# One block of bins for both image pairs in turn: head weights in six buffers, transfers in a fixed order, and the mix of images moved between blocks

## The chip, the cores and the metric

The kernel runs on one core of one Trainium2 chip. The metric is the device time in microseconds from launch to end; the figure quoted for a kernel is the median of several runs. Engines are named as in the profile: PE (TensorE matmuls), PEld (its weight loads), DVE (VectorE), ACT (ScalarE), POOL (GpSimd), SP (SyncE, here only the issuer of DMA transfers).

## The reference

Two layers follow one another, each added to its input. The first is a selective scan over a 48 × 48 image in four directions; the change does not touch it. The second is a spectral attention layer over an input of 4 batches × 48 images ("T") of 48 × 128 points with 32 heads. Cut to what matters:

```python
xa_n = inorm(x.reshape(B*T, 1, H, W))
k = fno_layer(xa_n, wK, wKs, bKs, (H//2, W//2))       # 32 heads each
q = fno_layer(xa_n, wQ, wQs, bQs, (H//2, W//2))
v = fno_layer(xa_n, wV, wVs, bVs, (H, W))
scores = einsum('bhtd,bhsd->bhts', qs, ks) / sqrt(d)
attn_w = softmax(scores, axis=-1)
out   = einsum('bhts,bhsd->bhtd', attn_w, vs)          # every head: a mix of the 48 images
projd = fno_layer(out, wP, wPs, bPs, (H, W))           # and back from 32 heads to one
attention = inorm(projd + xa)
...                                                    # two more spectral layers, norms, residual
# fno_layer(x): spectral part: multiply the low bins of rfft2(x) by complex weights, sum over heads;
#               plus a pointwise part: ws * x + bs
```

Since all of `v` and `projd` is linear in `xa_n`, the kernel never forms `v`. For each low bin n it computes, over heads h and images s, the sum of `attn[h,t,s] * g[h,n] * x[s,n]`, where `g` joins the weights of V and P, and x is the spectrum of the normalized image. The pointwise parts of V and P together are a 48 × 48 matrix for each batch, the "mix of images" (`a0_bd`): the sum over heads of `attn[h,t,s] * wPs[h] * wVs[h]`.

## The kernel before

The program is built with a tile framework. Tiles come from pools with a number of buffers per tag; a tile's first writer waits for the last readers of the buffer that it takes. Instructions issued through `nc` are put in order, engine by engine, by the framework's planner, which goes by program order and by its own estimate of when things become ready. Instructions issued through `on` (class `Ordered`, line 36) keep the order of the program among themselves on their engine; the helper's line 50 is therefore the line of all of them in the profile. Before the change `Ordered` knows TensorE, VectorE, ScalarE and GpSimd, not SyncE.

The second layer, `layer1` (line 735), begins with loads of constants and of the first layer's result. Line 916 opens the pool `l1_mid`, which holds the attention weights `attn_c` from the softmax to the end of the heads' stage. While statistics and the first transform run, `dgt` in DRAM is written (lines 1108 to 1115): the joint weights g of the 32 heads, for each of four blocks of 384 bins, real part, imaginary part and their sum. One block's transposes are copied by ScalarE into `gtt` (four tiles, one per block) and stored by SyncE. Later `keys` (line 1212) writes the images' spectrum to `dxt` in DRAM in the same blocks. The scores (line 1254) run at the same time; the softmax (lines 1273 to 1300) ends in transposes into `attn_c`, with (head, image s) on the partitions.

The heads' stage is lines 1308 to 1406. Its loops run over `pair` (2; a pair is two batches), `k` (4 blocks of 384 bins), `q` (3 groups of 16 images s) and `g` (4 groups of 8 heads). One (pair, k) is called a block here, one (pair, k, q) a step, one (pair, k, q, g) a group. The 128 partitions of a group are 16 images × 8 heads:

- `grep`: g of 8 heads at the block's bins, repeated for 16 images, 128 × 1152 values, one DMA transfer of 576 KB from `dgt` (line 1364). It is loaded at q = 0 and used by all three q of its block. The pool `l1_qg` has 4 buffers, the four g of one block.
- `xrep`: the spectrum of 16 images for both batches of the pair, each row repeated for 8 heads: two transfers of 576 KB from `dxt` (line 1356) for each step, two buffers.
- ScalarE copies two thirds of `grep` to PSUM (`gp`, line 1371); VectorE multiplies it by `xrep` into `v` (line 1373); GpSimd multiplies the last third into `v3` (line 1377; the profile calls it v too). Both have two buffers.
- TensorE multiplies by `attn_c` and sums over all q and g into three accumulators `acc` (line 1381): 6 matmuls of 64 columns a group, which the profile records as 12.

After 12 groups a block ends: ScalarE copies `acc[0]` to `s1` (1389), VectorE forms `zt` (1392 to 1394), TensorE transposes it in two lots of four (`pz`, 1399), ScalarE copies each to `z2` (1402). The accumulators have one buffer each, so the next block's matmuls need them read.

At the head of the stage, lines 1317 to 1327 load `wpv` (both pointwise weights of the heads, eight small transfers) and `mask` (three), and multiply the weights. `e_w` (1331, 1332) is built from them, and the mix of images is made for both pairs (1335 to 1348): 24 matmuls each into the PSUM tile of tag "tr", which `pz` uses as well, and a copy to `a0_bd`. Its result is first used in the next stage, the inverse transform.

The order of the transfers on SyncE's queue is the planner's. `grep` can be requested when the last step of the block before has used the buffer.

Of the kernel before, what the change touches and what calls it, by code (L numbers as in the profile page):

```python
# [10 lines left out]
F32 = mybir.dt.float32  # L11
# [8 lines left out]
B, T, H, W = 4, 48, 48, 128  # L20
# [9 lines left out]
NH = 32  # L30
# [5 lines left out]
class Ordered:  # L36


    def __init__(self, tc):
        for name in ("tensor", "vector", "scalar", "gpsimd"):  # L40
            setattr(self, name, _OrderedEngine(tc, getattr(tc.nc, name)))


# [691 lines left out]
def layer1(ctx, tc, io, x1_dram, out):  # L735
# [5 lines left out]
    nc = tc.nc  # L741
# [10 lines left out]
    on = Ordered(tc)  # L752
# [156 lines left out]
    NC = 384  # L909
# [7 lines left out]


    attn_c = pm.tile([128, B, 4, 3, 64], F32, name="attn_c")
    dxt = dram.tile([B, 4, T, 3 * NC], F32, name="dxt")  # L920


# [136 lines left out]
    with ExitStack() as ph:  # L1059
# [17 lines left out]
        with ExitStack() as pw:  # L1077
# [28 lines left out]
            on.vector.tensor_add(gw[:, :, 2], gw[:, :, 0], gw[:, :, 1])  # L1106

            for k in range(4):
                gt = q1.tile([NH, 3, NC], F32, name=f"gtt{k}")
                for c in range(3):  # L1110
                    p = ps_t.tile([128, 512], F32, tag="tr", name=f"pgt{k}_{c}")
                    for j in range(3):
                        on.tensor.transpose(p[0:NH, j * 128 : (j + 1) * 128], gw[:, 3 * k + j, c], ident)
                    on.scalar.copy(gt[:, c], p[0:NH, 0:NC])
                nc.sync.dma_start(dgt[k], gt.rearrange("h c n -> h (c n)"))
# [192 lines left out]
    with ExitStack() as ph:  # L1308
        p1 = ph.enter_context(tc.tile_pool(name="l1_q1", bufs=1))
        p2 = ph.enter_context(tc.tile_pool(name="l1_q2", bufs=2))  # L1310
        pg = ph.enter_context(tc.tile_pool(name="l1_qg", bufs=4))
        ps_t = ph.enter_context(tc.tile_pool(name="l1_qt", bufs=1, space=PSUM))
        ps_g = ph.enter_context(tc.tile_pool(name="l1_qp", bufs=2, space=PSUM))
        ps_y = ph.enter_context(tc.tile_pool(name="l1_qy", bufs=1, space=PSUM))


        wpv = p1.tile([128, 2, 4], F32, name="wpv")
        mask = p1.tile([128, 3, T], F32, name="mask")
        for c, n in enumerate(("wPs", "wVs")):
            w = io[n].rearrange("a b -> (a b)")  # L1320
            for g in range(4):
                nc.sync.dma_start(wpv[:, c, g : g + 1], w[8 * g : 8 * g + 8][None].to_broadcast([16, 8]))
        for q in range(3):
            nc.sync.dma_start(
                mask[:, q], io["c_ident"][16 * q : 16 * q + 16, 0:T][:, None].to_broadcast([16, 8, T])
            )
        nc.vector.tensor_mul(wpv[:, 0], wpv[:, 0], wpv[:, 1])
        e_w = []
        for g in range(4):
            e = p1.tile([128, 3, 3 * T], F32, tag=f"e_w{g}", name=f"e_w{g}")  # L1330
            nc.gpsimd.memset(e, 0.0)
            nc.vector.tensor_scalar(e[:, :, T : 2 * T], mask, wpv[:, 0, g : g + 1], None, ALU.mult)
            e_w.append(e)
        for pair in range(2):
            p = ps_t.tile([128, 512], F32, tag="tr", name=f"pa0{pair}")
            for i in range(2):
                o = p[0:96, i * T : (i + 1) * T]
                for gq in range(12):
                    g, q = divmod(gq, 3)
                    nc.tensor.matmul(  # L1340
                        o,
                        e_w[g][:, q, (1 - i) * T : (1 - i) * T + 96],
                        attn_c[:, 2 * pair + i, g, q, 0:T],
                        start=(i == 0 and gq == 0),
                        stop=(gq == 11),
                        skip_group_check=True,
                    )
            nc.scalar.copy(a0_bd[:, pair], p[0:96, 0:96])
        for pair in range(2):
            for k in range(4):  # L1350
                acc = [ps_y.tile([128, 512], F32, tag=f"acc{c}", name=f"acc{pair}_{k}_{c}") for c in range(3)]
                gr = []
                for q in range(3):
                    x = p2.tile([128, 2, 3, NC], F32, tag="xrep", name=f"xrep{pair}_{k}_{q}")
                    for b in range(2):
                        nc.sync.dma_start(
                            x[:, b].rearrange("p c n -> p (c n)"),
                            dxt[2 * pair + b, k, q * 16 : q * 16 + 16][:, None].to_broadcast([16, 8, 3 * NC]),
                        )
                    for g in range(4):  # L1360
                        t = f"{pair}_{k}_{q}_{g}"
                        if q == 0:
                            r = pg.tile([128, 3, NC], F32, tag="grep", name=f"grep{t}")
                            nc.sync.dma_start(
                                r.rearrange("p c n -> p (c n)"),
                                dgt[k, 8 * g : 8 * g + 8][None].to_broadcast([16, 8, 3 * NC]),
                            )
                            gr.append(r)
                        r = gr[g]
                        gp = ps_g.tile([128, 2, 512], F32, tag="gp", name=f"gp{t}")  # L1370
                        nc.scalar.copy(gp[:, :, 0:NC], r[:, 0:2])  # L1371
                        v = p2.tile([128, 2, 2, NC], F32, tag="v", name=f"v{t}")
# [6 lines left out]
                        for c in range(3):  # L1379
                            for b in range(2):  # L1380
# [4 lines left out]
                                    start=first,  # L1385
                                    stop=last,
                                )
                s1 = p2.tile([128, NC], F32, tag="s1", name=f"s1{pair}_{k}")
                nc.scalar.copy(s1, acc[0][:, 0:NC])  # L1389
                zt = p2.tile([128, 8, 2, 48], F32, tag="zt", name=f"zt{pair}_{k}")  # L1390
                a1, a2, a3 = (v[:, 0:NC].rearrange("p (k y) -> p k y", y=48) for v in (s1, acc[1], acc[2]))
# [3 lines left out]
                for k4 in range(2):  # L1395
                    p = ps_t.tile([128, 512], F32, tag="tr", name=f"pz{pair}_{k}_{k4}")
                    for i in range(4):
# [5 lines left out]
                        z2[pair][:, 8 * k + 4 * k4 : 8 * k + 4 * k4 + 4].rearrange("p k (b t) -> p k b t", b=2),  # L1403
                        p[0:96].rearrange("p (k b t) -> p k b t", b=2, t=64)[:, :, :, 0:T],
                    )
    mid.close()


# [553 lines left out]
```

## Time and profile before

| What | Value |
|---|---|
| Median of 3 runs | 5021.46 us (5015.16 to 5022.86) |
| Profiled execution, its own time | 5017.78 us |
| Its span, first to last instruction | 5016.0 us |
| Mean TensorE clock granted | 0.933 |
| Scores end, heads' stage begins | about 4441 us |
| First / last `acc` product of the heads' stage | 4477.6 / 4740.5 us |
| Busy over the span: PE, DVE, POOL, ACT | 83%, 83%, 80%, 59% |
| `xrep` transfers (576 KB each) | 48 |
| `grep` transfers (576 KB each) | 32 |

Times in the profile are microseconds from the first instruction. A row of instructions names line, engine, operation and output<-inputs; in brackets stands the idle time of the engine before it and what ended it. A row of waits gives who waited for whom, the total, how often, and the longest. The chain is the work that ended last, followed backwards through what released each piece. The clock is TensorE's granted clock as a share of full speed.

### The profile page before, as it was taken

To read this page: it belongs to the slowest core of one execution; us is meant where nothing else is said; L and a number is where in the kernel's file an instruction comes from. 1 tells how busy PE (TensorE), PEld (TensorE's weight loads), DVE (VectorE), ACT (ScalarE), POOL (GpSimd) and SP (SyncE) were. 2 spreads that over 40 slices of the span, in tenths; PEclk is the share of its full clock that TensorE was granted. 3 is DMA by queue.
4 is the path that set the end of the run, shared out by engine and by line. 5 is a ranking of instruction groups with operands and counts; after the bars stand their busy time and mean duration, and the time that the engine had idled before them with its cause. 6 is when DMAs were issued, how large, how long until landed. Compare 5 with 4: busy or idle time off the path is not lost.

```text
span 5016.0 us, 44268 instructions
## 1 busy us (share of the span) xinstructions
PE 4181.6 (83%) x12444; PEld 1916.5 (38%) x12444; DVE 4170.1 (83%) x2901; ACT 2953.2 (59%) x6608; POOL 3993.4 (80%) x2188
## 2 busy tenths in 40 slices
PE   6889898888798988887989888877788787888786
PEld 3334333333343333333433333333333332544443
DVE  3689998989899989898999898988999985556536
ACT  3666566766566666666666666665767663323334
POOL 4589998988899989898999898888999983246531
PEclk9989999999899999998999999998999998989877
DMA  2223232322232333232323332334333323147636
GB/s 54 74 89 101 91 116 89 104 89 97 92 107 94 116 89 104 88 102 90 106 95 117 92 102 91 98 101 96 106 106 102 103 91 88 40 97 172 160 99 151
DMA packets 278691, 501.01 MB, mean 100 GB/s; under 512 B 105940, under 2 KB 190036, under 8 KB 277868
## 3 DMA queue, kind: packets, MB, share of 16 engines
q1 hardware_dynamic: 272864, 495.11, 33.5%
q10 hardware_dynamic: 5580, 3.08, 0.2%
q8 instruction: 98, 1.61, 0.1%
q14 instruction: 149, 1.22, 0.1%
HBM read 462.93 MB, written 35.38 MB: 99 GB/s over the span
## 4 chain that ended last, share of the span: by engine, by line
DVE 17%; PE 15%; ACT 7%; issue 7%; POOL 3%; DMA 3%; SPq 1%; DVEq 0%; POOLq 0%; ACTq 0%
DVE h L50 12%; PE yp L50 4%; ACT da L50 3%; DVE db L50 3%; PE acc L1381 2%; POOL v L1377 1%; DMA grep<-dgt 1%; ACT L50 1%; PE sc L1254 1%; PE pi_p L50 1%; POOL db L50 1%; ACT dt L50 1%; POOL hc L50 1%; DVE m L50 1%; PE pe_m L50 0%
## 5 line engine op out<-in xcount | busy, mean ns | idle before, releaser
L50 POOL TENSOR_TENSOR hc<-h,cbc 128x960 f32<-128x960 f32 (+1 forms) x1280 | 2716.8, 2137 | 443.4 <-DVE h L50 328.5
L50 DVE TENSOR_TENSOR_SCAN h<-da,carry,db 128x961 f32<-128x961 f32 (+1 forms) x1280 | 2702.9, 2130 | 167.4 <-ACT carry L50 108.2
L50 ACT ACTIVATE da<-dt,a_neg 128x480 f32<-128x480 f32 (+1 forms) x2560 | 1660.9, 649 | 1188.1 <-DVE h L50 1143.2
L50 PE MATMUL yp<-hc,ident 128*128 128x480 f32 (+1 forms) x5120 | 2256.9, 568 | 19.4 <-POOL hc L50 19.2
L50 PEld LDWEIGHTS yp<-hc,ident 128*128 128x128 f32 x5120 | 999.1, 197 | 1381.4 <-issue 1003.7
L50 DVE TENSOR_TENSOR db<-du,pb 128x960 f32<-128x960 f32 (+1 forms) x960 | 1064.1, 1108 | 227.9 <-PE pb L50 172.0
L50 POOL TENSOR_TENSOR db<-du,bbc 128x960 f32<-128x960 f32 (+1 forms) x320 | 688.2, 2151 | 18.4 <-DMA bbc<-cd 9.6
L50 PE MATMUL pb<-bs,pick 112*128 112x480 bf16 (+1 forms) x960 | 357.7, 373 | 362.0 <-DVE db L50 360.3
L50 PE MATMUL pc<-pad,cdiag 128*128 128x480 f32 (+1 forms) x630 | 285.2, 564 | 8.3 <-ACT pad L50 8.3
L1377 POOL TENSOR_TENSOR v<-grep,xrep 128x768 f32<-128x768 f32 x96 | 174.4, 1819 | 117.9 <-PE acc L1381 60.8
L1381 PE MATMUL acc<-v,attn_c 128*64 128x384 f32 x1152 | 218.2, 513 | 36.5 <-ACT s L1389 32.1
L1373 DVE TENSOR_TENSOR v<-gp,xrep 128x1536 f32<-128x1536 f32 x96 | 168.1, 1757 | 88.7 <-PE acc L1381 41.3
L50 ACT COPY db<-carry 128x1 f32<-128x1 f32 x1280 | 226.0, 177 | 21.6 <-POOL db L50 15.1
L50 POOL TENSOR_TENSOR du<-dt,xc 128x480 f32<-128x480 f32 (+1 forms) x160 | 204.3, 1277 | 37.0 <-ACT dt L50 37.0
L50 PE MATMUL px<-xc,w_xp 128*112 128x480 f32 (+1 forms) x320 | 214.0, 756 | 16.9 <-ACT xc L50 13.3
L50 PEld LDWEIGHTS <-pick 112*128 112x128 bf16 x960 | 97.6, 102 | 329.1 <-issue 305.9
L50 ACT ACT_TABLE_LOAD x148 | 189.9, 1283 | 42.8 <-PE gv_l L50 19.5
L50 PE MATMUL pd<-xd,w_dt 8*128 8x480 f32 (+1 forms) x320 | 167.5, 603 | 40.5 <-ACT bs L50 24.7
L50 ACT COPY carry<-h 128x2 f32<-128x2 f32 x1024 | 192.6, 188 | 0.0
L50 PEld LDWEIGHTS pc<-pad,cdiag 128*128 128x128 f32 x630 | 122.6, 195 | 142.0 <-issue 115.5
L1371 ACT COPY gp<-grep 128x768 f32<-128x768 f32 x96 | 77.0, 803 | 157.3 <-DVE v L1373 79.7
L50 PE MATMUL yp<-y,ident 128*128 128x480 f32 (+1 forms) x240 | 167.6, 829 | 0.2
(366 smaller groups left out, 3162.5 us busy)
## 6 DMA issues: line engine op xcount, KB each, us to landing
cbc<-cd SPq DMA_DIRECT2D x512, 480.0 KB
bbc<-cd SPq DMA_DIRECT2D x256, 240.0 KB
cbc<-cd SPq DMA_DIRECT2D x128, 384.0 KB
xrep<-dxt SPq DMA_DIRECT2D x48, 576.0 KB
grep<-dgt SPq DMA_DIRECT2D x32, 576.0 KB
bbc<-cd SPq DMA_DIRECT2D x64, 192.0 KB
x<-in_xT SPq DMA_DIRECT2D x16, 288.0 KB
xr<-in_xT SPq DMA_DIRECT2D x16, 288.0 KB
```

Source lines behind the costliest of these rows:

```text
L50: return lambda *args, **kw: self._tc.keep_in_program_order(emit(*args, **kw))
L1254: nc.tensor.matmul(sc[64 * b : 64 * b + 64, g, 0 : 8 * T], qs[:, j, n, 2 * pair + b], f[b][:, 8 * g : 8 * g + 8], start=(jn == 0), stop=False,
L1371: nc.scalar.copy(gp[:, :, 0:NC], r[:, 0:2])
L1373: nc.vector.tensor_mul(v, gp[:, None, :, 0:NC].to_broadcast([128, 2, 2, NC]), x[:, :, 0:2])
L1377: nc.gpsimd.tensor_mul(v3, r[:, 2:3].to_broadcast([128, 2, NC]), x[:, :, 2])
L1381: nc.tensor.matmul(acc[c][64 * b : 64 * b + 64, 0:NC], attn_c[:, 2 * pair + b, g, q], v[:, b, c] if c < 2 else v3[:, b], start=first, stop ...
```

## The change

- `Ordered` also covers SyncE, so transfers can be issued in a fixed order.
- The loads of `wpv` and `mask` and the product `wpv` move to the layer's beginning, into the pool `l1_mid`.
- `gtt` shares two buffers instead of having four tiles. `s1` has one buffer instead of two.
- `grep` has six buffers instead of four.
- The loops are exchanged: k outside, pair inside. `grep` is loaded once for each k, for both pairs.
- `fetch(i + 1)` requests the next step's `xrep` at the start of step i. The `grep` of the next k follow in the same fixed order: two with the `xrep` of the last step of a k, two with that of the first step of the next. At the start all four follow the first `xrep`.
- The mix of images becomes a function called behind the block (k = 1) of each pair, which are the third and fourth of the eight blocks.

```diff
-        for name in ("tensor", "vector", "scalar", "gpsimd"):
+        for name in ("tensor", "vector", "scalar", "gpsimd", "sync"):
...
     attn_c = pm.tile([128, B, 4, 3, 64], F32, name="attn_c")
+    wpv = pm.tile([128, 2, 4], F32, name="wpv")
+    mask = pm.tile([128, 3, T], F32, name="mask")
+    for c, n in enumerate(("wPs", "wVs")):
+        w = io[n].rearrange("a b -> (a b)")
+        for g in range(4):
+            nc.sync.dma_start(wpv[:, c, g : g + 1], w[8 * g : 8 * g + 8][None].to_broadcast([16, 8]))
+    for q in range(3):
+        nc.sync.dma_start(mask[:, q], io["c_ident"][16 * q : 16 * q + 16, 0:T][:, None].to_broadcast([16, 8, T]))
+    nc.vector.tensor_mul(wpv[:, 0], wpv[:, 0], wpv[:, 1])
...
-                gt = q1.tile([NH, 3, NC], F32, name=f"gtt{k}")
+                gt = q1.tile([NH, 3, NC], F32, tag="gtt", name=f"gtt{k}", bufs=2)
...
-        pg = ph.enter_context(tc.tile_pool(name="l1_qg", bufs=4))
+        pg = ph.enter_context(tc.tile_pool(name="l1_qg", bufs=6))
...
-        wpv = p1.tile([128, 2, 4], F32, name="wpv")
-        mask = p1.tile([128, 3, T], F32, name="mask")
...
-        for pair in range(2):
+        def mix_of_images(pair):
             p = ps_t.tile([128, 512], F32, tag="tr", name=f"pa0{pair}")
...
-        for pair in range(2):
-            for k in range(4):
+        steps = [(k, pair, q) for k in range(4) for pair in range(2) for q in range(3)]
+        xs, gs = {}, {}
+
+        def fetch_weights(k, some):
+            for g in some:
+                r = pg.tile([128, 3, NC], F32, tag="grep", name=f"grep{k}_{g}")
+                on.sync.dma_start(
+                    r.rearrange("p c n -> p (c n)"),
+                    dgt[k, 8 * g : 8 * g + 8][None].to_broadcast([16, 8, 3 * NC]),
+                )
+                gs[k, g] = r
+
+        def fetch(i):
+            if i == len(steps):
+                return
+            k, pair, q = steps[i]
+            x = p2.tile([128, 2, 3, NC], F32, tag="xrep", name=f"xrep{pair}_{k}_{q}")
+            for b in range(2):
+                on.sync.dma_start(
+                    x[:, b].rearrange("p c n -> p (c n)"),
+                    dxt[2 * pair + b, k, q * 16 : q * 16 + 16][:, None].to_broadcast([16, 8, 3 * NC]),
+                )
+            xs[i] = x
+            if i == 0:
+                fetch_weights(0, range(4))
+            elif pair == 1 and q == 2 and k < 3:
+                fetch_weights(k + 1, range(2))
+            elif pair == 0 and q == 0:
+                fetch_weights(k, range(2, 4))
+
+        fetch(0)
+        for k in range(4):
+            for pair in range(2):
                 acc = [...]
-                gr = []
                 for q in range(3):
-                    x = p2.tile([128, 2, 3, NC], F32, tag="xrep", name=f"xrep{pair}_{k}_{q}")
-                    ... nc.sync.dma_start of both halves
+                    i = steps.index((k, pair, q))
+                    fetch(i + 1)
+                    x = xs.pop(i)
                     for g in range(4):
-                        if q == 0:
-                            r = pg.tile([128, 3, NC], F32, tag="grep", name=f"grep{t}")
-                            ... nc.sync.dma_start of the weights
-                        r = gr[g]
+                        r = gs[k, g]
...
-                s1 = p2.tile([128, NC], F32, tag="s1", name=f"s1{pair}_{k}")
+                s1 = p2.tile([128, NC], F32, tag="s1", name=f"s1{pair}_{k}", bufs=1)
...
+                if k == 1:
+                    mix_of_images(pair)
```

More of the change, by code (lines that the diff above doesn't have):

```diff
@@ L919, in layer1 @@
     attn_c = pm.tile([128, B, 4, 3, 64], F32, name="attn_c")
+    wpv = pm.tile([128, 2, 4], F32, name="wpv")
[5 more added lines that the diff above has]
+    for q in range(3):
+        nc.sync.dma_start(
+            mask[:, q], io["c_ident"][16 * q : 16 * q + 16, 0:T][:, None].to_broadcast([16, 8, T])
+        )
+    nc.vector.tensor_mul(wpv[:, 0], wpv[:, 0], wpv[:, 1])
     dxt = dram.tile([B, 4, T, 3 * NC], F32, name="dxt")
@@ L1314, in layer1 @@
         ps_y = ph.enter_context(tc.tile_pool(name="l1_qy", bufs=1, space=PSUM))
-        wpv = p1.tile([128, 2, 4], F32, name="wpv")
-        mask = p1.tile([128, 3, T], F32, name="mask")
[L1319 to L1327, printed above, removed]
         e_w = []
@@ new lines, in fetch @@
+        def fetch(i):
[7 more added lines that the diff above has]
+                    dxt[2 * pair + b, k, q * 16 : q * 16 + 16][:, None].to_broadcast([16, 8, 3 * NC]),
+                )
+            xs[i] = x
[5 more added lines that the diff above has]
+                fetch_weights(k, range(2, 4))
@@ L1351, in layer1 @@
+        fetch(0)
+        for k in range(4):
+            for pair in range(2):
                 acc = [ps_y.tile([128, 512], F32, tag=f"acc{c}", name=f"acc{pair}_{k}_{c}") for c in range(3)]
-                gr = []
                 for q in range(3):
-                    x = p2.tile([128, 2, 3, NC], F32, tag="xrep", name=f"xrep{pair}_{k}_{q}")
[L1355 to L1359, printed above, removed]
+                    i = steps.index((k, pair, q))
+                    fetch(i + 1)
+                    x = xs.pop(i)
@@ L1360, in layer1 @@
                     for g in range(4):
                         t = f"{pair}_{k}_{q}_{g}"
-                        if q == 0:
-                            r = pg.tile([128, 3, NC], F32, tag="grep", name=f"grep{t}")
[L1364 to L1368, printed above, removed]
-                        r = gr[g]
+                        r = gs[k, g]
```

## The prediction

> **What bounds the kernel now.** I read the page first: its slices put the changed code, lines 1309 to 1406, in the 36th to 38th of forty. The stage runs from the last scores (about 4441 us) to the last product of heads (4740.5 us). Everything before it, 88% of the span, is not touched but for two small moves. Inside the stage I read the waits, the chain, the busy time by stretch, and the queues.
>
> The waits between 4441 and 4745 us (engine and line, what it waited for: total, times, longest):
>
> ```profile
> ACT gp L1371 <- DMA grep<-dgt: 77.6, 28, 7.0
> POOL v L1377 <- PE acc L1381: 60.8, 13, 7.8
> PE acc L1381 <- ACT s L1389: 32.1, 7, 5.1
> POOL v L1377 <- DMA xrep<-dxt: 23.8, 1, 23.8
> ```
>
> The second buffer of head weights is the story: 28 waits on `grep` are four for each of the seven boundaries between blocks. TensorE itself waits seven times for the copy `s1`, which is queued on ScalarE behind two `gp` copies that wait for `grep`. The chain at one boundary shows the order (start, us, what):
>
> ```profile
> 4631.14 1.84 POOL v L1377
> ...
> 4632.99 8.89 DMA grep<-dgt
> ...
> 4641.97 0.80 ACT gp L1371
> 4642.77 0.42 ACT s L1389
> ...
> 4643.21 0.55 DVE zt L1392
> 4643.76 1.68 DVE v L1373
> ...
> 4645.49 2.82 PE acc L1381 x4
> 4648.31 1.02 PE pz L1399 x4
> 4649.33 0.87 PE acc L1381 x4
> 4650.20 0.57 PE pz L1399 x4
> ```
>
> A buffer is free only when the last third of a block has used it; its transfer then takes 8.89 us. TensorE's own timeline gives the length of a boundary:
>
> ```profile
> 4616.59 22.14 PE L1381 MATMUL acc<-v,attn_c 128*64 128x384 f32 x132
> 4643.23 1.55 PE L1381 MATMUL acc<-v,attn_c 128*64 128x384 f32 x4 [4.50 <-ACT s L1389]
> ```
>
> The steady run ends at 4616.59 + 22.14 = 4638.73 and the next begins at 4650.70: 11.97 us, of which 12 matmuls, 1.94 us, are the work of one group of heads. Within a run one group takes 1.935 us (the DVE multiplies start that far apart), bound by TensorE: 12 records of 0.161 us. The blocks end at 4504.70 first and 4740.54 last: 235.84 / 7 = 33.69 us each.
>
> Stretches (us, busy and count on PE, PEld, DVE, ACT, POOL, then TensorE clock, DMA share, GB/s):
>
> ```profile
> 4461.00:4478.00 17.00, 16.14 (x98) 15.81 (x100) 4.59 (x6) 0.82 (x4) 3.58 (x2) 0.50 0.67 155
> 4490.00:4504.00 14.00, 14.00 (x89) 6.44 (x86) 10.46 (x6) 3.98 (x5) 11.60 (x7) 1.00 0.74 176
> 4598.00:4604.00 6.00, 6.00 (x40) 2.73 (x38) 4.75 (x3) 1.21 (x2) 5.16 (x3) 1.00 1.03 241
> 4643.20:4647.00 3.80, 3.06 (x7) 0.99 (x8) 3.24 (x4) 0.80 (x1) 0.65 (x1) 0.50 1.03 233
> ```
>
> Read three things: the mix of images (first row) runs at clock 0.50; the DMA engines are full at 241 GB/s, so one 576 KB transfer takes 589824 / 241000 = 2.45 us; and after the wait at a boundary the clock is 0.50 (last row).
>
> **The change, part by part.**
>
> *Start of the stage.* On VectorE the product `wpv` stands ahead of the last softmax:
>
> ```profile
> 4457.96 0.16 DVE L1327 TENSOR_TENSOR wpv<-wpv 128x4 f32<-128x4 f32 x1 [4.68 <-DMA mask<-in_c_ident]
> ```
>
> The first `xrep` transfers wait for that softmax (SyncE: VectorE's `sn`, then the transpose) and issue at 4460.87. Without the 4.68 us they issue at 4456.2. Then, however, the fixed order puts all four `grep` behind them, two of which were issued at 4440.94 before. Data begin some 2.4 us after issue (a pair issued at 4519.78 landed at 4527.13: 7.35, less two times 2.45). So `xrep` is complete at 4463.5 and `grep` at 4466.0, 4468.4, 4470.9 and 4473.4, the second `xrep` at 4478.3. The loads pace the first four groups. The fifth `v` starts at 4478.4 and its matmuls at 4480.1; now that `v` starts at 4486.50 and its matmuls at 4488.2. The mix (4461.5 to 4477.7) is no longer ahead. Eight groups later block 0 ends at 4480.1 + 8 × 1.935 = 4495.6 instead of 4504.7: **−9.1**.
>
> *Boundaries.* The same four `grep` serve both pairs, so 16 transfers go (32 to 16, together with 48 `xrep` 64 instead of 80), and of the next block of bins two are loaded two steps early into buffers five and six. With nothing to wait for, the chain from the block's end E is: `s1` done at E − 0.8, while VectorE ends the next `v` at E − 0.2; L1392 to E + 0.4, `v` to E + 2.1, L1393 and L1394 to E + 3.3 (0.55, 1.75, 0.54, 0.56 from the rows), four transposes, four matmuls, copy, four transposes: 2.7 at full clock, between the 2.8 (4512.35 to 4515.15) and the 4.2 of the trace. Sum **6.0 us** in place of 11.8 on average. Bounds: 4.2, if VectorE takes the three `zt` instructions first; 9.3, if the 8.0 us from `s1` to the steady run (4608.6 to 4616.6) stay as they are. I take 6.0, since the half clock there follows the idle 4.5 us that go. The run between takes 11 × 1.935 = 21.3, and 0.3 for `xrep` that come late, as the 22.14 shows now. So 27.6 for 33.69, seven times: **−42.6**.
>
> *`xrep`.* One load takes 7.35 to 7.85 us from the release to landing (4519.78 to 4527.13; 4587.91 to 4595.75). With two buffers, a step starts no earlier than its second predecessor's start + 7.64 (POOL ends its fourth product: 3 × 1.935 + 1.83) + 7.35 to 7.85, so 7.5 to 7.75 us per step against TensorE's 7.74. It is just hidden. Here the Trainium skill speaks otherwise: *DMA: Bandwidth & Descriptors*, section "Anatomy of one DMA", fits 2.0 us plus bytes / 436e3 (for the GpSimd path), so 4.7 us for the pair, and no step would ever wait. By the row the two `grep` fetched along are felt: at a change of k the `xrep` queues behind them, landing 17.2 us after a release (2.4 + 6 × 2.46) where 15.5 is free. I take the row: +1.4 for each of three, one of them hidden under the mix: **+2.8**. By the rule 0.
>
> *Mix of images.* Its 96 matmul records go behind blocks 2 and 3 (2 × 48), on TensorE ahead of the next block's matmuls; ScalarE's `a0_bd` copy (0.23) waits for it with the next `gp` copies behind. Nothing covers it. At full clock the weight loads of 96 columns set it: 48 × 0.097 (the `pz` loads) = 4.7; the trace has 7.92. *TensorE: Matmul & The Clock Gate*, Part 1, says that some 3.4 us of sustained activity release the clock. The first row above differs: 16 us of back-to-back small matmuls left it at 0.50. So these do not count as enough activity, and behind a block the mix may lose the full clock and hand half clock to the next block (4477.6 to about 4482 ran at half: 2.2 lost). By the page 2 × 4.7 = 9.4; by the row up to 2 × 10.1. I take 7.0 each: **+14.0**.
>
> *Small edits.* Eight `wpv` and three `mask` transfers move on SyncE's queue from 4445 to 4453 to the layer's start (4196 to 4209), 11 × 0.55 = 6 us; behind them stand `w_p`, `w_v` and `d48`, first used at 4279, and `a2` loads from 4243: no cost. If VectorE meets the `wpv` product before they land, as now, it costs up to 4.7 in the chain of statistics there; I take 0. `gtt` with two buffers: the seventh copy (4291.08, on the chain) waits for the first store, issued at 4288.81; a comparable store took 2.58 us (`dxt`, 4433.11), so it lands at about 4291.7: **+0.7**. `s1` with one buffer: its readers ended 20 us earlier; nothing.
>
> **Sum.** −9.1 − 42.6 + 2.8 + 14.0 + 0.7 = −34.2. The profiled execution took 5017.78 (span 5016.0): 4983.6. Its time is 3.7 below the median of the three runs, within their 5015 to 5023. Between 4983.6 and 5021.5 − 34.2 = 4987.3 I say **4985**.
>
> **Rivals.**
>
> *Weights still late* (0.12). If the third and fourth `grep`, requested when step (k, pair 1, last) gives up its buffers, hold up each change of k as now, only the four boundaries within a k shrink: the 42.6 becomes 24.4, and the result 5003. For it: the 8.89 us of a `grep`. Against: the first two groups give 4 us, and the boundary more, before the third is used.
>
> *The boundary's own chain stays* (0.14): at 9.3 us, seven times 3.3 come back: 5008. For it: VectorE's order there, with a `v` between the `zt`. Against: clock and wait go together.
>
> *Mix hidden, boundary at 4.2* (0.10): 12.6 and some 8 more: 4964. For it: TensorE idles in each boundary. Against: the mix stands behind the transposes.
>
> *Slower: `xrep` paces every step* (0.03). One step takes 5.0 + t, t being one transfer. The stage breaks even when 24 × (5.0 + t) reaches today's 263 us (4477.6 to 4740.5) and the 9.1 won at the start: t = 6.3 us, 94 GB/s; 7.0 us would give 5037. The row says 2.45 at 241 GB/s, and the total falls by a fifth.
>
> **How the numbers follow.** The forecast has 0.61; its own range is 4972 to 4998 (boundary ± 1, mix 4.7 to 10.1, `wpv` up to 4.7). The upper end of 8 in 10 goes to 5004, into the first two rivals, the lower to 4965. A measurement tells 0.2%, 10 us. The rivals at 5003 and 5008 are still faster by more than that; about a sixth of the two lies within 10 us of today: same 0.04, slower 0.03, faster 0.93.
>
> **What would show it.** Of `grep` 16 transfers, and hardly a wait of ScalarE for them; boundary gaps on TensorE of about 6 us with the clock near 1; block 0 ending at about 4496 and the stage at about 4706; the mix between blocks at 5 to 8 us each. The prediction is wrong if the steps run clearly over 7.8 us, if `xrep` becomes the wait that ends last, or if the order of the stage around it moves.

## The result and the profile after

The changed kernel takes 4989.5 us in the median (4983.0 to 4990.6), the kernel before 5021.9 beside it: ratio 0.9936, 95% interval 0.9924 to 0.9949, so 32 us or 0.64% faster. The forecast was 4985. The profiled execution took 4989.15 us with a span of 4987.4, 28.6 less than before; the mean clock is 0.931. That the total came out near its forecast is in part luck. Four terms were well off, `xrep` and `wpv` by 11 and 7 us too low, the mix and `gtt` by 7 and 6 us too high, and their errors nearly cancel.

The waits of the heads' stage in the changed kernel, 4440 to 4720 us (engine and line, what it waited for: total, times, longest):

```profile
POOL v L1400 <- PE acc L1404: 48.7, 16, 7.0
...
ACT gp L1394 <- DMA grep<-dgt: 32.1, 10, 9.6
...
DVE v L1396 <- DMA xrep<-dxt: 10.6, 11, 3.3
...
ACT s L1412 <- PE acc L1404: 8.1, 8, 4.3
```

The 28 waits for `grep` (77.6 us) have become ten (32.1 us), four of them at the start, and TensorE's waits for `s1` (32.1 us) are gone; `s1` now waits for TensorE, as it should. TensorE's timeline shows both kinds of boundary. First one within a block of bins, then a change of k, then the boundary that carries the mix:

```profile
4502.74 1.50 PE L1404 MATMUL acc<-v,attn_c 128*64 128x384 f32 x4 [1.10 <-DVE v L1396]
...
4506.12 22.14 PE L1404 MATMUL acc<-v,attn_c 128*64 128x384 f32 x132
4530.88 1.40 PE L1404 MATMUL acc<-v,attn_c 128*64 128x384 f32 x4 [2.62 <-DVE v L1396]
4532.91 2.82 PE L1404 MATMUL acc<-v,attn_c 128*64 128x384 f32 x4 [0.64 <-DVE v L1396]
4535.66 1.09 PE L1422 MATMUL pz<-ident,zt 128*96 128x128 f32 x4
...
4538.64 22.79 PE L1404 MATMUL acc<-v,attn_c 128*64 128x384 f32 x136
4562.52 1.50 PE L1404 MATMUL acc<-v,attn_c 128*64 128x384 f32 x4 [1.09 <-DVE v L1396]
...
4567.33 4.28 PE L1340 MATMUL pa<-attn_c,e_w 128*96 128x48 f32 x48
```

The run before the change of k ends at 4506.12 + 22.14 = 4528.26, the next begins at 4538.64: 10.4 us, nearly the 12 of before. Here and below the length of a block is the distance between two `s1` copies on ScalarE, if nothing else is said (in the changed kernel a block's last product ends about 1.25 us behind the start of its copy). The seven are 27.2, 32.5, 31.6, 35.2, 27.5, 32.1 and 27.7 us; before, the ends of the blocks were 33.8 apart on average. Of the seven the second, fourth and sixth are the changes of k; the third and fourth carry a mix. At a change of k the chain reads (start, us, what):

```profile
4519.21 9.64 DMA xrep<-dxt
...
4528.97 0.06 DVE v L1396
...
4530.65 0.54 DVE zt L1415
4531.19 1.68 DVE v L1396
...
4532.91 2.82 PE acc L1404 x4
4535.73 1.02 PE pz L1422 x4
4536.75 1.38 PE acc L1404 x4
```

What now comes late is `xrep`, not `grep`. SyncE's queue shows why:

```profile
4510.91 1.16 SPq L50 DMA_DIRECT2D xrep<-dxt  x2
4512.11 1.24 SPq L50 DMA_DIRECT2D grep<-dgt  x2
4518.65 1.16 SPq L50 DMA_DIRECT2D xrep<-dxt  x2
```

The `xrep` of the new k stands behind two `grep` of the new k and lands 9.64 us after it was issued; it took 7.35 to 7.85 before, and 6.7 to 6.9 at the other steps of this kernel that stand on the chain. The DMA engines are full from the time the first data move until it lands (us, busy and count on PE, PEld, DVE, ACT, POOL, then mean clock, DMA share, GB/s):

```profile
4513.30:4528.85 15.55, 14.96 (x93) 10.34 (x88) 11.06 (x7) 6.12 (x8) 12.41 (x7) 1.00 1.03 246
```

TensorE's clock at the first groups, at the boundary within a k, behind the late `xrep` and in the mix (the same columns):

```profile
4472.45:4479.88 7.43, 6.55 (x20) 2.46 (x22) 3.13 (x3) 2.42 (x3) 3.61 (x2) 0.50 1.03 234
4502.00:4506.20 4.20, 3.46 (x18) 1.52 (x20) 2.19 (x4) 1.28 (x2) 0.97 (x1) 1.00 0.75 176
4531.10:4537.90 6.80, 6.16 (x16) 1.69 (x12) 2.78 (x4) 2.09 (x3) 1.49 (x1) 0.50 0.77 184
4567.40:4571.60 4.20, 4.20 (x50) 4.15 (x52) 0.00 (x0) 0.69 (x1) 1.31 (x1) 1.00 0.02 4
```

Behind the late `xrep` (a pause of 2.62 us) the clock is 0.50 for 6.8 us; at the boundary within a k (a pause of 1.10 us) it stays at 1.00, and the mix runs at 1.00.

Ahead of the stage, where I had put nothing, VectorE shows this:

```profile
4207.07 0.66 DVE L50 TENSOR_TENSOR ws<-ws,pr 128x480 f32<-128x480 f32 x1 [3.56 <-PE pr L50]
4214.67 0.16 DVE L932 TENSOR_TENSOR wpv<-wpv 128x4 f32<-128x4 f32 x1 [6.95 <-DMA mask<-in_c_ident]
4214.75 1.48 DVE L50 BATCH_NORM_STATS2 st<-x_in 128x6 f32<-128x384 f32 x3
```

The product `wpv` stands ahead of the layer's first statistics and waits 6.95 us for the moved loads; the first `pm` product of TensorE goes from 4217.5 to 4225.7. Yet the scores begin at 4342.3, only 0.7 later than before: something in between gave the delay back. The scores end 3.9 later (their last weight load starts at 4444.0 instead of 4440.1; this is the "end of the scores" below), the last `acc` comes 26.3 earlier.

### The profile page after: what moved, and what is told of

Same layout as the page of the kernel before. It is cut to its first block, busy times and chain, and to the rows that moved or that the text cites. A ratio compares the mean times of both kernels' runs of the same rounds, so it can differ in the third digit from the quotient of the medians.

```text
span 4987.4 us, 44228 instructions
## 1 busy us (share of the span) xinstructions
PE 4176.6 (84%) x12444; PEld 1913.7 (38%) x12444; DVE 4169.9 (84%) x2901; ACT 2964.0 (59%) x6608; POOL 3992.7 (80%) x2188
## 3 DMA queue, kind: packets, MB, share of 16 engines
q1 hardware_dynamic: 270560, 485.67, 32.5%
q14 instruction: 150, 1.22, 0.1%
## 4 chain that ended last, share of the span: by engine, by line
DVE 18%; PE 15%; issue 7%; ACT 7%; POOL 3%; DMA 2%; SPq 1%; DVEq 0%; POOLq 0%; ACTq 0%
DVE h L50 12%; PE yp L50 4%; ACT da L50 3%; DVE db L50 3%; PE acc L1404 2%; ACT L50 1%; PE sc L1267 1%; POOL v L1400 1%; POOL db L50 1%; PE pi_p L50 1%; DMA xrep<-dxt 1%; ACT dt L50 1%; POOL hc L50 1%; ACT ws L50 1%; PE px L50 1%
## 5 line engine op out<-in xcount | busy, mean ns | idle before, releaser
L50 POOL TENSOR_TENSOR db<-du,bbc 128x960 f32<-128x960 f32 (+1 forms) x320 | 688.9, 2153 | 17.2 <-DMA d_m<-in_wK 8.5
L1404 PE MATMUL acc<-v,attn_c 128*64 128x384 f32 x1152 | 211.5, 504 | 26.7 <-DVE v L1396 13.6
L1404 PEld LDWEIGHTS acc<-v,attn_c 128*64 128x64 f32 x1152 | 119.2, 139 | 108.5 <-issue 53.7
```

The lines of the kernel that those rows point to most:

```text
L50: return lambda *args, **kw: self._tc.keep_in_program_order(emit(*args, **kw))
L1404: nc.tensor.matmul(acc[c][64 * b : 64 * b + 64, 0:NC], attn_c[:, 2 * pair + b, g, q], v[:, b, c] if c < 2 else v3[:, b], start=first, stop ...
```

## The experiments

Every kernel was timed beside the kernel before on its own chip; medians of before were 5018.7 to 5021.9. Where a few microseconds decide, I read the trace from a common point, since the same code ahead of it can end some 4 us apart from run to run (the first `pm` of `layer1` at 4216.1 with the loops exchanged, at 4220.6 with `gtt` alone, which do not differ up to there).

### Four `gtt` tiles again

```diff
-                gt = q1.tile([NH, 3, NC], F32, tag="gtt", name=f"gtt{k}", bufs=2)
+                gt = q1.tile([NH, 3, NC], F32, name=f"gtt{k}")
```

> The changed kernel with four gtt tiles again (one per block of bins). Its list of instructions then stands as in the kernel before on ScalarE, GpSimd and TensorE up to the scores; with two buffers the planner put the first xt copy behind the first psel copies and two f products ahead of xt on GpSimd. Theory A (the order of the planner, not the wait of the store, is what gtt changed): the scores take 3.2 us less, pgt and pxn 0.7 less, but TensorE idles for the xt copies ahead of psel and psel runs at half clock again (+5.4): net +1.5, about 4991, with the clock near 0.5 at psel. Rival B (the clock at psel is a matter of chance or of the late statistics): only the gains stay, -4, 4985. Rival C (my prediction: gtt is worth 0.7): 4988.5 with psel and scores as in the changed kernel.

4998.0 us (4993.8 to 5000.1), ratio 0.9957 (0.9942 to 0.9972): 8 us slower than the changed kernel. Theory A was right in kind, short in size, and both others fell. `psel` on TensorE (the products between the first transform and the scores) runs from 4322.9 to 4336.4, against 4319.6 to 4329.8. Ahead of it the idle time of before is back, and with it the lower clock. Three stretches of this kernel:

```profile
4318.00:4324.00 6.00, 4.60 (x41) 2.71 (x39) 3.54 (x24) 2.98 (x6) 1.03 (x1) 1.00 0.09 18
4321.72:4326.45 4.73, 4.73 (x51) 2.27 (x52) 0.18 (x1) 1.30 (x5) 1.03 (x1) 1.00 0.23 50
4326.50:4333.25 6.75, 6.75 (x82) 3.88 (x83) 0.00 (x0) 3.38 (x11) 0.00 (x0) 0.50 0.00 0
```

the kernel before at the same place:

```profile
4311.55:4325.15 13.60, 13.60 (x112) 6.24 (x116) 0.14 (x1) 3.75 (x12) 0.99 (x1) 0.50 0.08 18
```

and the changed kernel:

```profile
4318.00:4324.00 6.00, 6.00 (x71) 2.95 (x72) 2.17 (x18) 4.16 (x10) 0.00 (x0) 1.00 0.01 3
4324.00:4330.00 6.00, 6.00 (x154) 3.18 (x148) 0.00 (x0) 5.88 (x19) 0.00 (x0) 1.00 0.02 3
```

The breaks of 0.84 and 0.56 us in TensorE's work are followed by half clock: for 6.8 us here, beginning 4.7 us behind the second break, and for 13.6 us in the kernel before, beginning right behind it. Why the two differ is not shown. But the scores did not become 3.2 us shorter: 101.3 from their first to their last weight load with the old order, 101.7 in the changed kernel, 98.5 before. That part of theory A is not borne out.

### `gtt` in two buffers, nothing else

```diff
-                gt = q1.tile([NH, 3, NC], F32, name=f"gtt{k}")
+                gt = q1.tile([NH, 3, NC], F32, tag="gtt", name=f"gtt{k}", bufs=2)
```

> The kernel before with one edit of the change: gtt in two buffers. Up to the scores ScalarE, GpSimd and TensorE then have the changed kernel's order (the first xt copy behind the first psel copies), without its late statistics. Theory A (that order is worth 5 to 7 us, because TensorE then doesn't idle ahead of psel and keeps its clock): psel from its first to its last product 10 us instead of 16 at full clock, scores' first product about 6 us earlier; of this the scores give back 0 to 3: -3 to -6, 5014. Rival B (the clock at psel hangs on the late statistics of the changed kernel): psel takes 16 us as before, 0 to +1, 5019.

5013.7 us (5005.3 to 5020.2) against 5018.7, ratio 0.9989 (0.9981 to 0.9998). The step that I had booked as a wait of 0.7 us is a gain of 5 (between 1 and 9.5 by the interval). `psel` takes 10.3 us instead of 15.6 from first to last product. Its longest run, in the kernel before and in this one:

```profile
4320.45 9.01 PE L1169 MATMUL psel<-a_x,sel 96*32 96x192 f32 x158
```

```profile
4316.77 6.70 PE L1169 MATMUL psel<-a_x,sel 96*32 96x192 f32 x158
```

The scores give 4.2 back (102.7 for 98.5). The planner, given two buffers, orders the work differently: on ScalarE the first `xt` copy moves behind the first `psel` copy, so TensorE comes to `psel` without having waited for `xt` copies.

### The product `wpv` back at the stage's head

```diff
-    nc.vector.tensor_mul(wpv[:, 0], wpv[:, 0], wpv[:, 1])
     dxt = dram.tile([B, 4, T, 3 * NC], F32, name="dxt")
...
+        nc.vector.tensor_mul(wpv[:, 0], wpv[:, 0], wpv[:, 1])
         e_w = []
```

> The changed kernel with the product wpv back at the head of the heads' stage, its loads still at the layer's beginning; no other engine's order differs. Theory A: the 7.1 us that VectorE waited for the mask ahead of the statistics pass through to the end: pm at about 4218.6 instead of 4225.7, end at about 4982 (-7). Rival B: they are absorbed (psel at half clock, or the a2 loads or w_p set the end of that part): 0, 4989. The head of the heads' stage must not get a new wait by either, since mask is long there.

4984.3 us (4981.7 to 4988.8), ratio 0.9932 (0.9917 to 0.9947): faster than the changed kernel by 5 us by the medians and 7.5 by the spans, but only by 2 by the ratios, whose intervals overlap. The times alone do not settle it; the trace does. The timeline of VectorE:

```profile
4207.17 2.85 DVE L50 BATCH_NORM_STATS2 st<-x_in 128x6 f32<-128x384 f32 x6
...
4214.20 0.17 DVE L1327 TENSOR_TENSOR wpv<-wpv 128x4 f32<-128x4 f32 x1 [1.12 <-DMA mask<-in_c_ident]
```

The planner still placed the product early, but behind most of the statistics, and 1.12 us of the wait is left. `pm` starts 6.4 us sooner (0.5 of it because layer 0 ended sooner in this run), `psel` 7.1, the scores 7.1, the first `acc` 7.1, and the last `acc` 6.4: the delay passed through to the end, and rival B falls.

### Head weights spread over two steps

```diff
-            elif pair == 1 and q == 2 and k < 3:
-                fetch_weights(k + 1, range(2))
+            elif (pair, q) in ((0, 2), (1, 0)) and k < 3:
+                fetch_weights(k + 1, [pair])
```

> The changed kernel with the first two grep of the next k fetched one by one, behind the xrep of (k, pair 0, q 2) and of (k, pair 1, q 0), instead of both behind that of (k, pair 1, q 2). Theory A (xrep lands late at a change of k because it is queued behind two grep, and the clock then falls): the three changes of k cost as the boundaries within a k, blocks of 32.1 to 32.5 become 27.6 to 28.5 (and 35.2 with the mix becomes 31.5): -12, 4977. Rival B (the third and fourth grep, or the accumulators' chain, hold the change of k anyway): at most -3, 4986. Rival C (half: the late xrep is gone, grep 2 and 3 wait as now): -6, 4983.

4978.8 us (4977.8 to 4984.9), ratio 0.9923 (0.9907 to 0.9940). Blocks: 27.4, 28.7, 31.6, 32.6, 27.3, 28.2, 27.3. The three changes of k lose 3.8, 2.6 and 3.9. At the first of them:

```profile
4506.46 23.16 PE L1404 MATMUL acc<-v,attn_c 128*64 128x384 f32 x136
4530.79 1.50 PE L1404 MATMUL acc<-v,attn_c 128*64 128x384 f32 x4 [1.17 <-DVE v L1396]
4532.22 0.64 PE L1422 MATMUL pz<-ident,zt 128*96 128x128 f32 x4
```

The break is that of a boundary within a k (1.17), and the transposes take 0.64 instead of 1.09. The clock stays full from the first boundary to the last:

```profile
4502.00:4704.00 202.00, 192.10 (x1156) 118.40 (x1156) 154.48 (x104) 75.44 (x104) 150.56 (x83) 1.00 0.61 145
```

So the late `xrep`, with the fall of the clock behind it, was most of the cost: at the first and third change of k 3.8 and 3.9 of some 5 us. What is left, 28.7 and 28.2 against 27.3, is not explained; the third and fourth `grep`, still fetched as in the change, hold up that much at most.

### The planner's order in place of the fixed one

```diff
-                on.sync.dma_start(
+                nc.sync.dma_start(
```

at both transfers of the stage.

> The changed kernel with the transfers of the heads' stage in the planner's order instead of the fixed one; six buffers and the exchanged loops stay. The planner then puts the first xrep behind two grep and one more store of the spectrum, and at each change of k the first two grep behind the xrep of the next k instead of ahead of it. Theory A (what is queued ahead of an xrep decides): xrep is no longer late at a change of k, but all four grep land behind it, 2.45 us apart: ScalarE waits for grep instead; within 4 us of the changed kernel, 4986 to 4993. Rival B (the fixed order is worth a good part of the gain): +10 or more, 5000.

4974.4 us (4974.1 to 4975.4), ratio 0.9914 (0.9898 to 0.9931): 11 us faster than the changed kernel by the ratios, 15 by the medians, which none of my theories had. Theory A's mechanism was the right one, with a sign I had not seen through. Six buffers are free at the start, and the planner uses all of them at once:

```profile
4444.56 1.89 SPq L1358 DMA_DIRECT2D grep<-dgt  x3
...
4449.40 1.98 SPq L1358 DMA_DIRECT2D grep<-dgt  x3
4460.18 58.77 SPq L1370 DMA_DIRECT2D xrep<-dxt  x14
```

All four `grep` of the first k and two of the second are under way before the softmax frees the first `xrep`, where the fixed order held them back behind it. TensorE's first run is then not broken up:

```profile
4471.41 25.85 PE L1404 MATMUL acc<-v,attn_c 128*64 128x384 f32 x144 [11.30 <-POOL v L1400]
```

Block 0's `s1` comes 3.7 us sooner (4496.1 for 4499.8), and the blocks are 30.1, 28.6, 31.6, 31.8, 27.3, 28.1, 27.2: 9.1 us less over the seven. The first, 30.1, has an `xrep` 1.8 us late and half clock from 4500.1 to 4503.6, the only fall of the clock between blocks here. ScalarE waits 10.6 us for `grep` in all.

### Loops exchanged, nothing else

The kernel before with its own four buffers, planner's order, mix and `wpv`:

```diff
-        for pair in range(2):
-            for k in range(4):
+        gs = {}
+        for k in range(4):
+            for pair in range(2):
...
-                        if q == 0:
+                        if pair == 0 and q == 0:
```

> The kernel before with only the loops exchanged (k outside, pair inside, grep loaded once for each k); four buffers, the planner's order of transfers, the mix and wpv at the stage's head. Theory A (the gain is the wait for grep at a boundary, one transfer fewer than blocks): four of seven boundaries shrink by 6.1, the three changes of k stay at about 33.7: 5017.8 - 24.4 = 4993 in the profiled time, 4997 against the median. Rival B (six buffers and the fixed order carry the gain): within 6 us of the kernel before. Rival C (xrep, then, is late at every step since the planner's order does not look ahead): slower than 5000.

4993.5 us (4989.8 to 4996.3), ratio 0.9949 (0.9934 to 0.9964): 25.4 us faster than before, against 24.4 expected. The blocks' last products end 27.3, 34.9, 28.1, 34.0, 27.3, 34.4 and 27.3 us apart: short within a k, as long as ever at a change. TensorE's first boundary within a k, and the first change of k:

```profile
4505.09 1.50 PE L1381 MATMUL acc<-v,attn_c 128*64 128x384 f32 x4 [1.11 <-DVE v L1373]
...
4535.71 1.55 PE L1381 MATMUL acc<-v,attn_c 128*64 128x384 f32 x4 [5.10 <-ACT s L1389]
```

An edit of a few lines carries four fifths of the whole change's gain; the buffers, the fixed order and the moves together bring 4 us net by the medians, 6.5 by the ratios.

### The mix of images at the stage's head, and left out

```diff
+        for pair in range(2):
+            mix_of_images(pair)
         fetch(0)
...
-                if k == 1:
-                    mix_of_images(pair)
```

> The changed kernel with the mix of images for both pairs back at the head of the heads' stage; everything else as changed. Theory A (at the head TensorE waits for the first xrep and grep until 4472 anyway, so most of the mix's 16 us there are covered, while between blocks 4.2 us each and some 3 to 4 us more behind them are not): first acc about 4 us later, of which 1.8 are won back since the groups are then no longer paced by the loads; the blocks with the mix shrink by 8.5 together: -6, 4983. Rival B (my prediction's reading: the mix at the head costs its 16 us of half clock in full, less the 9.1 of the loads): first acc 7 us later, middle -14 at most, between -1.5 and -7. Rival C: 0, since whatever is won in the middle is lost at the start with the clock at half.

4987.2 us (4984.5 to 4988.9), ratio 0.9936 (0.9921 to 0.9951): the changed kernel's. Counted from the end of the scores the last `acc` comes 4.0 us sooner (first `acc` 4.5 later, then 8.5 won), but the times do not show it, so the verdict stays open between theory A and rival C. The clock is plain, though. At the head, two stretches of this kernel:

```profile
4459.00:4468.00 9.00, 8.94 (x54) 8.78 (x54) 2.53 (x6) 1.78 (x5) 0.00 (x0) 0.50 0.01 2
4468.00:4476.20 8.20, 7.92 (x48) 7.75 (x48) 0.00 (x0) 0.22 (x1) 0.00 (x0) 0.50 0.99 235
```

The same matmuls that run at 1.00 between blocks run 17 us at 0.50 here, where TensorE comes from the breaks of the softmax (4.47 and 1.22 us).

The second kernel leaves the mix out (its result is zero):

```diff
-                if k == 1:
-                    mix_of_images(pair)
...
+        nc.gpsimd.memset(a0_bd, 0.0)
         fetch(0)
```

> The changed kernel without the mix of images (its result is set to zero: the pointwise part of the attention is left out, the output is not the reference's; the weights e_w are still made). Theory A (the two mixes at full clock cost their own 4.2 us each and nearly nothing more): -8.5, 4981, blocks three and four 27.6 to 28 and the change of k without the mix's extra. Rival B (my prediction: 7.0 each with the clock lost behind them): -14, 4975. Rival C (one of them is hidden under the late xrep at the change of k): -5, 4984.

4982.3 us (4976.3 to 4989.1), ratio 0.9927 (0.9911 to 0.9943). The two stretches with the mix take 28.1 and 32.1 instead of 31.6 and 35.2: a mix costs 3.5 and 3.1 us, less than its own 4.28; I take the rest to lie under the wait for the next `v`, which no run isolates. Over all seven blocks this kernel is only 4.8 us shorter, since its last change of k took 34.0 instead of 32.1, with a wait of 4.4 us for `xrep`. By the times theory A and rival C cannot be told apart (7 us by the medians, 4.5 by the ratios, whose intervals overlap); the 3.1 us at the change of k say that the mix there is not hidden, against rival C.

### The three `zt` together behind one `v`

VectorE's order is fixed for `v` and `zt`, with `v` one group ahead:

```diff
-                        nc.vector.tensor_mul(
-                            v, gp[:, None, :, 0:NC].to_broadcast([128, 2, 2, NC]), x[:, :, 0:2]
-                        )
+                        if (i, g) != (len(steps) - 1, 3):
+                            multiply(*((i, g + 1) if g < 3 else (i + 1, 0)))
...
-                nc.vector.tensor_sub(zt[:, :, 0], a1, a2)
+                on.vector.tensor_sub(zt[:, :, 0], a1, a2)
```

and likewise the other two; `multiply` issues `gp`, `v` and `v3` of one group, `v` through `on.vector`.

> The changed kernel with VectorE's order fixed at a block's end: one v of the next block, then the three zt, then the second v; now the second v stands between the first and the second zt. GpSimd, SyncE and the transfers stay. Theory A (the accumulators are read 1.7 us sooner, so TensorE's pause at each of seven boundaries shrinks by that): -12, 4977; boundaries within a k of 4.3 us instead of 6. Rival B (the second v is then the late one, and TensorE waits for it instead): 0 to -3. Rival C (at a change of k xrep sets the end, so only the four within a k shrink): -7, 4982.

4975.1 us (4971.3 to 4978.5), ratio 0.9912 (0.9897 to 0.9927). Blocks: 25.6, 30.1, 31.3, 34.4, 25.7, 28.4, 25.8. Within a k 1.6 to 1.9 us less, as theory A had it; the total of seven is 12.5 less. At the first and third change of k it is 2.4 and 3.7 less, so rival C falls too.

### Weights of the first block ahead of its `xrep`

```diff
+            if i == 0:
+                fetch_weights(0, range(4))
             x = p2.tile([128, 2, 3, NC], F32, tag="xrep", name=f"xrep{pair}_{k}_{q}")
...
-            if i == 0:
-                fetch_weights(0, range(4))
-            elif pair == 1 and q == 2 and k < 3:
+            if pair == 1 and q == 2 and k < 3:
```

> The changed kernel with the four grep of the first block ahead of the first xrep in the fixed order, instead of behind it. They need nothing of the softmax but free buffers. Theory A (all four land before the first xrep, and the first groups are no longer paced by the loads at 2.5 us each): first acc at about 4470 instead of 4472.4, block 0 ends 4 us earlier, 4985. Rival B (the buffers of the third and fourth grep are free only after the softmax, so xrep behind them is issued later): +2 to +5, 4993. Rival C (clock at half in this stretch sets the pace, not the loads): 0.

4985.5 us (4981.3 to 4987.7), ratio 0.9932 (0.9915 to 0.9949). With the first branch gone, step 0 also met the last one, so `grep` 2 and 3 of the first block were fetched again behind the first `xrep`: two transfers more than I meant to have. The times do not tell it from the changed kernel (4 us by the medians, 2 by the ratios, overlapping). Even so, counted from the end of the scores, the first `acc` is 2.0 us sooner, the end of block 0 4.1, as theory A had it, and the last `acc` 5.2. By the trace rivals B and C fall.

### Together

The product `wpv` late, the weights spread, and `zt` together:

> The changed kernel with three edits together, each run alone before: the product wpv at the stage's head, the grep of the next k spread over two steps, the three zt behind one v. Singly -6.5, -11 and -13 in the traces. Theory A (they act in different places; at a change of k the last two overlap by some 3 us in all): -27, 4962. Rival B (with the boundaries short, xrep paces the steps, since a step then has less slack): -20, 4969.

4963.5 us (4962.1 to 4967.6), ratio 0.9893 (0.9879 to 0.9908): 26 us ahead of the changed kernel by the medians, as theory A had it, but 22 by the ratios, which is nearer to rival B. Blocks 25.6, 26.2, 31.0, 31.6, 25.6, 26.2, 25.7: changes of k cost 0.6 more than the others. VectorE waits for `xrep` 6.5 us in all and never more than 1.1, so the cause that rival B names is not seen. The clock does not fall between blocks any more:

```profile
4475.40:4689.30 213.90, 211.52 (x1288) 119.14 (x1284) 175.22 (x116) 84.19 (x116) 169.62 (x93) 1.00 0.67 157
```

The same with the first four `grep` ahead of the first `xrep`, each fetched once (`elif i and pair == 0 and q == 0:` in the last branch):

> The same three edits and the four grep of the first block ahead of the first xrep, each fetched once (in b4_greps_first the third and fourth were fetched a second time behind the first xrep: two transfers more than meant). Theory A (the loads of the first groups are then out of the way): first acc 3 us earlier after the scores' end and the first four groups 1.94 us apart instead of 2.5: -4 against the three edits alone, 4958. Rival B (the buffers of the third and fourth grep are free only after the softmax): 0 or slower, 4962 to 4966.

4959.8 us (4956.1 to 4961.0), ratio 0.9883 (0.9869 to 0.9898): the fastest, 59 us ahead of the kernel before on the same chip and ahead of the change by 27 (by the ratios) to 30 (by the medians). From the end of the scores to the first `acc` it is 26.9 us instead of 29.3 with the three edits alone, and the run starts unbroken:

```profile
4463.48 18.42 PE L1411 MATMUL acc<-v,attn_c 128*64 128x384 f32 x96 [10.52 <-POOL v L1393]
```

## Why the prediction was right, and where it was not

**Start of the stage, −9.1: right in kind.** Counted from the end of the scores, the first `acc` comes 9.1 us sooner (37.5 to 28.4). Block 0 ends 7.6 sooner (64.6 to 57.0). The loads pace the first groups, as worked out: with them out of the way block 0 ends 4.1 sooner still. I left out the clock, 0.50 until 4479.9; that it accounts for the missing 1.5 us is likely, not isolated.

**Boundaries, 33.69 to 27.6: right within a k.** Three such blocks take 27.2 to 27.7, and the fourth 28.1 in the kernel that leaves the mix out. From the end of a block to the steady run it takes 5.1 to 5.5 us where I had 6.0, and the run 22.1 to 22.3 where I had 21.6: two small errors that cancel. The cause was right: with the loops exchanged and nothing else, the wait for `grep` goes within a k and stays at a change, and the clock stays full at a boundary without it. That the chain could be shorter, the lower bound of 4.2, was right too (25.6 with `zt` together), but it takes another edit. (The 33.69 was read a little short: the last block ended at 4741.17, not at 4740.54, which makes it 33.8.)

**`xrep` at a change of k, +2.8: the step that failed most.** The three take 32.5, 32.1 and 32.1 us (the second from the kernel without the mix) against the 27.6 that I had for a block: 4.6 each, some +14. The mechanism was the one named. Two terms were off. The pair landed 17.9 us after its predecessor's issue (4510.91 to 4528.85) where I had 17.2, and the `v` that waits was due 15.1 behind it (2.3 us ahead of the block's end, as at the boundary before), not 15.5: 2.9 late. And I had no term for the clock: from that `v` to the steady run it takes 9.67 us (4528.97 to 4538.64) instead of 7.34 (4498.78 to 4506.12), 2.3 more, with the clock at 0.50 for 6.8 us. Nor was one of the three hidden under the mix. By the fit in the Trainium skill's *DMA: Bandwidth & Descriptors*, section "Anatomy of one DMA", which is for the GpSimd path, the six transfers would take some 10 us (an estimate, as the 4.7 for a pair was: 2.0 + 6 × 589824 / 436e3) and there would be no wait at all; the row was the better guide and still too kind.

**Mix of images, +14.0: too dear by half.** It costs 6.6 for both. I took 7.0 each, between 4.7 at full clock and the row's 10.1. On TensorE it took 4.28 each, at clock 1.00, and the clock behind it stayed at 1.00. The step that failed is the one from a row in which TensorE had come in at half clock to a place where it comes in at full clock: 17 us of these small matmuls did not bring a full clock about, but in the 4.28 us that one mix lasts none was lost. Whether a longer row of them would keep it, no run shows. The rule in the Trainium skill's *TensorE: Matmul & The Clock Gate*, Part 1, that some 3.4 us of sustained activity release the clock, does not hold for the 17 us at the stage's head; the mix between blocks does not test it.

**`gtt`, +0.7: wrong sign.** Alone it gains 5.0; taken out of the change it costs 8. I looked for the wait that a missing buffer brings (and its sum comes to 0.3, since 4288.81 + 2.58 is 4291.4) and forgot that the planner orders by when it thinks things become ready: with the other order TensorE's breaks ahead of `psel` go, and the half clock behind them.

**`wpv` moved, 0: wrong, though its price was named.** I wrote that it "costs up to 4.7 in the chain of statistics" if VectorE met it early. VectorE did, and waited 6.95: the eleven loads are issued from 4202.82 to 4211.4, where I had 4196 to 4209, and the 4.7, read off another place, was too small. To take 0 without a reason was the step that failed.

**The sum.** From the end of the scores: −7.6 − 42.6 + 14 + 6.6 = −29.6, measured −30.2 to the last `acc`, where the prediction had −34.9 for these terms. Ahead of it: +1.1 from layer 0's own run to run difference, +7.1 from `wpv`, and −4.3 in the rest, in which `gtt`'s gain at `psel` is set against longer scores. Behind it the tail is 2.3 us shorter than in the profile of before (275.3 to 273.0 from the start of the last `acc`); the kernel with `gtt` alone, whose code there is that of before, took 272.2, so I take it for a difference between runs and not for an effect of the change. So it sums to 28.6.

**The rivals.** "Weights still late" named the place that stayed slow, the changes of k, and the wrong transfer: with the third and fourth `grep` as they were and only the first two moved away from `xrep`, most of the cost went. "The boundary's own chain stays" fell at 27.2. "Mix hidden" was half right on the mix. "`xrep` paces every step" fell: VectorE waits for it 11 times, 10.6 us in all, 6.4 of them at the first and the third change of k.

**The signs that the prediction named.** There were 16 `grep` transfers, but ScalarE still waits 32.1 us for them, where I had "hardly a wait": 14.8 for the first four, 17.3 at the changes of k. Block 0 ended at 4501.0 and not at 4496, the stage at 4714.9 and not at 4706 (in both, 3.9 us of the difference is the later end of the scores), and the mix cost 3.5 and 3.1 us, not 5 to 8 each. Two of the signs that it is wrong did come: at the changes of k `xrep` is the wait that ends last, and the order ahead of the stage moved, at `psel`. The number was right in spite of them.

**What stays open.** The scores take 3 us longer in the changed kernel than before, and also with `gtt` back in four tiles (101.3), so the order that `gtt` brings does not explain it alone. With `gtt` alone they take 4 us longer. I did not isolate what does it.

## What to carry to other kernels

Ask of each transfer what stands ahead of it in its queue when it is needed, not only whether the engines can carry the load: here the weights fetched "early" were fetched in front of the one transfer that was due. A pause can cost twice on TensorE, once as idle time and once as the lower clock behind it: the 2.6 us at a change of k did, the 1.1 us at a boundary within a k did not. So read the clock behind each pause and put a price on both. And where a planner orders the work, an edit to a buffer count far from the stage can be worth more than the wait that it adds: compare the orders on every engine before you book it at its wait.

## What the runs showed of the hardware

- The same 48-column matmuls, back to back, ran 17 us at clock 0.50 where TensorE came to them from pauses, and at 1.00 (4.28 us for 48) where it came from full blocks. Only the first of the two stretches is long.
- Two breaks of 0.84 and 0.56 us in otherwise steady work (waiting for ScalarE's `xt` copies) were followed by half clock, for 13.6 us in the kernel before and for 6.8 us with four `gtt` put back; where the other order leaves no break, in the changed kernel and with `gtt` alone, it stayed at 1.00.
- A pause of 2.62 us at a change of k was followed by 6.8 us at clock 0.50; behind the 1.10 us of a boundary within a k the clock stayed at 1.00, and with `xrep` no longer late it did so through all 202 us from the first boundary to the last.
- Six transfers in sequence to SyncE's queue, two `xrep`, two `grep`, two `xrep`, landed 17.9 us after the first was issued, with the engines full at 246 GB/s for the last 15.5 us of it.
